# Moving five of the 24 depthwise-tap products of a band from VectorE to ScalarE and to adding transfers, in the last image of a two-layer convolution kernel

## The chip, the cores and the metric

The kernel runs on one core of one Trainium2 chip. The metric is the device time of one execution in microseconds (us), taken as the median of several runs. The engines are called by the profile's names: PE (TensorE, matrix products), ACT (ScalarE), DVE (VectorE), POOL (GpSimd), SP (SyncE, which here only issues transfers), and the DMA engines that move data.

## The reference

Eight images of 384 channels and 64 x 64 pixels pass through two layers, each added to its own input. Layer 0 is group normalisation and linear attention over the pixels. Layer 1, where the change lies, is

```
t  = w_in @ groupnorm(x)                       # 384 x 384, per pixel
t  = irfft2(rfft2(t, 8x8 patches) * filter)    # per channel
t  = depthwise 3x3 convolution of t with w_dw  # per channel, zero padding
x1, x2 = first and second half of the channels
x  = x + w_out @ (gelu(x1) * x2)
```

Everything is float32.

## The kernel before

**Tiling.** The channels are three tiles of 128 partitions (index `m`). An image is cut into eight bands of eight rows, so a band of one channel tile is 128 x 512 numbers. Layer 0 of image b + 1 and layer 1 of image b run interleaved through most of the program. The last image has nothing left to interleave: its layer 1 is a stage of its own, lines 1130 to 1150, and the change acts only there.

**One band of that stage** (loop variable `j`):

1. `expand_filter` (L688): PE makes `pi` (the product with `w_in`, L694), ACT copies it to `ht` (L701), PE makes the transform `pd` (L708), and DVE multiplies it by the filter into `tf` (L716).
2. `normalised` (L322): ACT prepares the next band's input `hf`.
3. `back_transform` (L719): PE makes `pb` from `tf` (L729), ACT copies it into `ring[j % 2]` (L739), a tile of ten rows of 66 columns for each channel. Row 0 is copied from the band above (L744), and row 9 of the band above is filled from this one (L745).
4. `first_taps` (L772): ACT makes the product of tap 0 for each `m` (L776) and so starts the band's sums, the tile `dw` (two buffers, pool `taps`).
5. `contract(b, j - 2)` (L852): PE makes `pw` from `gated` (L820, L831) and ACT copies it to `y` (L845). One transfer issued by POOL adds `y` to the output in memory (L850).
6. `taps(b, j - 1)` (L789): for the band before, DVE does the other eight taps of each `m` in `tile_taps` (L781), one instruction each (L787): `dw[m] = ring[m, shifted] * weight + dw[m]`. Taps 0 to 5 read rows 0 to 8 of the ring tile; taps 6 to 8 also read row 9, and so have to wait for the next band.
7. `gate_taps` (L795): gelu on ACT (L799, L803) and products on DVE (L800, L804) turn the sums into `gated`, a single buffer, which contraction j - 1 reads one iteration later.

In bands 6 and 7 (`on_array`, L751) the taps of `m` = 2 are done by PE as products with diagonal matrices (`ptap`, L764), and DVE does 16 taps.

**Order of the work.** Each engine works through its own queue strictly in order. The order inside a queue is fixed when the program is built: a planner plays the program through with its own estimates of every duration, and whenever an engine is free it takes the ready instruction that stands first in the program text. Scratch tiles (`w_tile`, nine buffers) and PSUM tiles (eight) are handed out in the order of the text. Where a real duration differs from the estimate, the engine does not choose again: it waits at the head of its queue.

Outside this stage, `tile_taps` is called by `last_band` and by `taps` through `depthwise_gate` for the other images.

Of the kernel before, what the change touches and what calls it, by code (L numbers as in the profile page):

```python
# [11 lines left out]
AF = mybir.ActivationFunctionType  # L12
ALU = mybir.AluOpType

P = 128
C = 384
CT = 3
# [100 lines left out]
def conv_blocks_kernel(ctx: ExitStack, tc: tile.TileContext, a: dict, out: bass.AP, nb: int):  # L118
    nc = tc.nc
# [9 lines left out]
    def ps_tile(name):  # L129
        return psum.tile([P, 512], F32, tag="ps", name=name)  # L130

    def w_tile(shape, name):
        return work.tile(shape, F32, tag="w", name=name)
# [13 lines left out]
    def store_x(b, j):  # L147

        if (b, j) != (nb - 1, NBAND - 1):
            nc.sync.dma_start(x_out[b][:, :, j * BT : (j + 1) * BT], xt.pop((b, j)))  # L150
# [79 lines left out]
    def const_tile(shape, name, src, queue=nc.scalar):  # L230
        t = const.tile(shape, F32, tag=name, name=name)
        queue.dma_start(t, src)
        return t
# [13 lines left out]
    scale = HD ** -0.5  # L247
# [9 lines left out]
    ring = []  # L257
# [64 lines left out]
    def normalised(b, j, params, order, name):  # L322

        rs, nb_ = params
        h = w_tile([P, CT, BT], f"h{name}_{b}_{j}")
        for t in range(CT):
            dst, src = h[:, t, :], xt[b, j][:, t, :]
            if order is not None:
                blocks, width = order
                dst = dst.rearrange("p (b r c) -> p r b c", b=blocks, r=8, c=width)  # L330
                src = src.rearrange("p (r b c) -> p r b c", b=blocks, r=8, c=width)
            nc.scalar.activation(dst, src, AF.Identity, bias=nb_[:, t : t + 1], scale=rs[:, t : t + 1])  # L332
        return h
# [354 lines left out]
    def expand_filter(b, j, h, done):  # L688
        ht = w_tile([P, 4, C], f"ht_{b}_{j}")
        tf = w_tile([P, 4, C], f"tf_{b}_{j}")  # L690
        for i in range(4):
            p_ = ps_tile(f"pi_{b}_{j}_{i}")
            for t in range(CT):
                nc.tensor.matmul(  # L694
                    p_[:, :C],
                    h[:, t, i * P : (i + 1) * P],
                    w_in[:, t, :],
                    start=(t == 0),
                    stop=(t == CT - 1),
                )  # L700
            nc.scalar.copy(ht[:, i, :], p_[:, :C])  # L701
        yield

        for s in range(2):
            p_ = [ps_tile(f"pd_{b}_{j}_{2 * s + i}") for i in range(2)]
            for above in range(2):
                for i in range(2):
                    nc.tensor.matmul(  # L708
                        p_[i][halves[above], :C],
                        dft[halves[i], :],  # L710
                        ht[halves[i], 2 * s + above, :],
                        start=True,
                        stop=True,
                    )
            for i in range(2):
                nc.vector.tensor_mul(tf[:, 2 * s + i, :], p_[i][:, :C], filt)  # L716
        done.append(tf)

    def back_transform(b, j, tf):  # L719
        t = ring[j % 2]  # L720
        for m0, m1 in ((0, 2), (2, 3)):


            ps = [ps_tile(f"pb_{b}_{j}_{m0}_{u}").rearrange("p (m s i n) -> p m s i n", m=2, s=2, i=2) for u in range(2)]
            for m in range(m0, m1):
                for k in range(4):
                    for c in range(2):
                        for u, half in enumerate(halves):
                            nc.tensor.matmul(  # L729
                                ps[u][halves[c], m - m0, k // 2, k % 2],  # L730
                                tf[half, k, m * P + 64 * c : m * P + 64 * c + 64],
                                idft[half, :],
                                start=True,
                                stop=True,
                            )
            for m in range(m0, m1):
                rows = t[:, m, 1:9, 1 : W + 1].rearrange("p r (s u i c) -> p u r s i c", s=2, u=2, i=2)
                for u in range(2):
                    nc.scalar.copy(rows[:, u], ps[u][:, m - m0].rearrange("p s i (r c) -> p r s i c", r=8))  # L739
        if j == 0:  # L740
            nc.gpsimd.memset(t[:, :, 0, :], 0.0)
        else:
            before = ring[(j - 1) % 2]
            nc.scalar.copy(t[:, :, 0, :], before[:, :, 8, :])  # L744
            nc.scalar.copy(before[:, :, 9, :], t[:, :, 1, :])  # L745
        if j == NBAND - 1:
            nc.gpsimd.memset(t[:, :, 9, :], 0.0)

    dw, dw_pe, diagonals = {}, {}, []

    def on_array(b, j):  # L751

        return b == nb - 1 and j >= NBAND - 2
# [7 lines left out]
    def array_taps(b, j, ks):  # L761

        for k in ks:
            nc.tensor.matmul(  # L764
                dw_pe[b, j].rearrange("p (r w) -> p r w", w=W),
                diagonals[0][:, k * P : (k + 1) * P],
                ring[j % 2][:, 2, k // 3 : k // 3 + 8, k % 3 : k % 3 + W],
                start=(k == 0),
                stop=(k == 8),
            )  # L770

    def first_taps(b, j):  # L772

        acc = dw[b, j] = taps_pool.tile([P, CT, 8, W], F32, tag="dw", name=f"dw_{b}_{j}")
        for m in range(CT - on_array(b, j)):
            nc.scalar.activation(acc[:, m], ring[j % 2][:, m, 0:8, 0:W], AF.Copy, scale=w_dw[:, m, 0:1])  # L776
        if on_array(b, j):
            dw_pe[b, j] = ps_tile(f"ptap_{b}_{j}")
            array_taps(b, j, range(9 if j == NBAND - 1 else 6))

    def tile_taps(b, j, m):  # L781

        t, acc = ring[j % 2], dw[b, j]
        for k in range(1, 9):
            src = t[:, m, k // 3 : k // 3 + 8, k % 3 : k % 3 + W]
            wd = w_dw[:, m, k : k + 1]
            nc.vector.scalar_tensor_tensor(acc[:, m], src, wd, acc[:, m], ALU.mult, ALU.add)  # L787

    def taps(b, j):  # L789
        if on_array(b, j) and j < NBAND - 1:  # L790
            array_taps(b, j, range(6, 9))
        for m in range(CT - on_array(b, j)):
            tile_taps(b, j, m)

    def gate_taps(b, j):  # L795
        g = gated
        af = dw.pop((b, j)).rearrange("p t r w -> p t (r w)")
        last = dw_pe.pop((b, j)) if on_array(b, j) else af[:, 2, :]
        nc.scalar.activation(g[:, :BT], af[:, 0, :], AF.Gelu)  # L799
        nc.vector.tensor_mul(g[:, :BT], g[:, :BT], af[:, 1, :])  # L800
        for h, gelu in enumerate((gelu2[64:P, :], g[64:P, BT:])):
            of = slice(h * HT, (h + 1) * HT)
            nc.scalar.activation(gelu, last[0:64, of], AF.Gelu)  # L803
            nc.vector.tensor_mul(g[halves[h], BT:], gelu, last[64:P, of])  # L804
# [47 lines left out]
    def contract(b, j):  # L852
        run(contraction(b, j))
# [18 lines left out]
    def run(*chains):  # L872

        chains = list(chains)
        while chains:
            chains = [c for c in chains if next(c, chains) is not chains]
# [135 lines left out]
    for c0, at, n in QRUNS:  # L1012

        t, p0, quarter, first = at // P, at % P, c0 // QC, c0 % QC
# [13 lines left out]
    w_dw = const_tile([P, CT, 9], "w_dw", a["w_dw"], nc.sync)  # L1028
# [31 lines left out]
    def last_band(b):  # L1060

        for m in range(CT):
            tile_taps(b, NBAND - 1, m)
            if m == CT - 1:
                gate_taps(b, NBAND - 1)
            yield
        if b + 1 < nb - 1:
            contract(b, NBAND - 1)

    before_last, late = nothing, iter(())  # L1070
    for b in range(nb):
# [19 lines left out]
        for j in range(NBAND):  # L1091
# [19 lines left out]
            some(2 * items)  # L1111
            back_transform(b, j, tf[0])
            first_taps(b, j)
            some(items)
            if j > 1:
# [15 lines left out]
    b = nb - 1  # L1131
    h = ahead
    for j in range(NBAND):
        tf = []
        layer1 = expand_filter(b, j, h, tf)
        run(layer1)
        store_x(b, j)
        if j < NBAND - 1:
            h = normalised(b, j + 1, params, (8, 8), "f")
        back_transform(b, j, tf[0])  # L1140
        first_taps(b, j)
        if j >= 2:
            contract(b, j - 2)
        if j >= 1:
            taps(b, j - 1)
            gate_taps(b, j - 1)
# [45 lines left out]
```

## Time and profile before

| what | value |
|---|---|
| time before, median of 3 runs | 3383.83 us (3383.71 to 3386.06) |
| the profiled execution's own time | 3384.08 us |
| its span, from first to last instruction | 3382.3 us |
| PE busy over the span | 3300.6 us (98%) |
| DVE busy | 2786.1 us (82%) |
| ACT busy | 1965.9 us (58%) |
| POOL busy | 142.6 us (4%) |
| L787 on DVE, whole program | 1520 instructions, 748 ns mean |
| first `pi` of the last image's layer 1 | 3203.78 us |
| first tap product of band 0 on ACT (L776) | 3219.83 us |
| the same of band 7 | 3350.67 us |

In the profile an instruction is named by its line, its engine and what it writes and reads (`dw<-ring,w_dw,dw`). Busy shares are averages over the whole span. The last image's stage is only the last 180 us, so what bounds it has to be read from views that are limited to it.

### The profile page before, as it was taken

What the parts mean: (1) busy time and instruction counts of PE and PEld (TensorE: products, weight loads), DVE (VectorE), ACT (ScalarE), POOL (GpSimd) and SP (SyncE); (2) the same over time, 40 slices, a digit from 0 to 9 for tenths busy, and PEclk for the clock granted to TensorE, in tenths of its full rate; (3) what the DMA queues carried; (4) which work ended last, traced back from release to release, by engine and by line L of the source; (5) the groups of instructions that cost most, each with busy time, mean ns of one, the idle gap of its engine ahead of it and who ended that gap; (6) DMA issues with size and microseconds to landing.
All of it is one profiled execution on the core that took longest, in us unless ns stands there. A gap on an engine that the chain in (4) does not pass through costs nothing.

```text
span 3382.3 us, 53235 instructions
## 1 busy us (share of the span) xinstructions
PE 3300.6 (98%) x21356; PEld 1850.2 (55%) x21356; DVE 2786.1 (82%) x4438; ACT 1965.9 (58%) x3849; POOL 142.6 (4%) x247
## 2 busy tenths in 40 slices
PE   8999999999999999999999999999999999999987
PEld 5544565456654566545664456644566445664454
DVE  6587889968899688996889868898788977989598
ACT  4445675556665576655675556655576555555553
POOL 0000001000010000100001000010000100000000
PEclk9999999999999999999999999999999999999999
DMA  6323244242442423424334333433233431324113
GB/s 223 112 94 108 75 101 111 100 138 56 111 115 94 135 74 87 123 101 120 85 89 122 102 115 76 111 109 116 92 96 93 120 114 54 85 70 112 57 24 53
DMA packets 149483, 336.01 MB, mean 99 GB/s; under 512 B 27140, under 2 KB 38388, under 8 KB 141044
## 3 DMA queue, kind: packets, MB, share of 16 engines
q1 hardware_dynamic: 123844, 282.85, 24.9%
q0 software_dynamic: 25200, 49.55, 10.1%
q8 instruction: 168, 2.75, 0.3%
q14 instruction: 79, 0.65, 0.1%
q10 hardware_dynamic: 192, 0.21, 0.0%
HBM read 232.70 MB, written 99.88 MB: 98 GB/s over the span
## 4 chain that ended last, share of the span: by engine, by line
PE 82%; DVE 14%; ACT 2%; issue 1%; DMA 0%; SPq 0%; DVEq 0%; ACTq 0%
PE pf L676 15%; PE pk L438 14%; PE pi L694 13%; PE pv L454 13%; PE pq L597 9%; DVE dw L787 6%; PE pw L820 4%; PE pb L729 3%; PE pd L708 2%; PE pw L831 2%; PE acc L470 2%; PE acc L483 2%; PE pn L635 1%; DVE qc L610 1%; DVE qc L339 1%
## 5 line engine op out<-in xcount | busy, mean ns | idle before, releaser
L787 DVE SCALAR_TENSOR_TENSOR dw<-ring,w_dw,dw 128x512 f32<-128x512 f32 x1520 | 1063.1, 748 | 244.2 <-ACT ring L745 205.4
L597 PE MATMUL pq<-x,wq 128*128 128x512 f32 x1152 | 529.0, 607 | 27.9 <-ACT qs L624 16.9
L438 PE MATMUL pk<-wk,x 128*128 128x384 f32 x1536 | 543.6, 495 | 0.0
L694 PE MATMUL pi<-w_in,hf 128*128 128x384 f32 x1536 | 514.4, 492 | 1.3 <-ACT hf L332 1.3
L676 PE MATMUL pf<-qc,mt 128*128 128x512 f32 x1152 | 512.8, 598 | 0.2
L454 PE MATMUL pv<-wv,x 128*128 128x384 f32 x1344 | 470.0, 488 | 0.0
L694 PEld LDWEIGHTS pi<-w_in,hf 128*128 128x128 f32 x1536 | 288.4, 191 | 196.0 <-issue 3.8
L438 PEld LDWEIGHTS pk<-wk,x 128*128 128x128 f32 x1536 | 282.9, 190 | 204.6 <-issue 31.3
L597 PEld LDWEIGHTS pq<-x,wq 128*128 128x128 f32 x1152 | 213.0, 192 | 278.9 <-issue 241.1
L461 ACT COPY v<-pv 128x384 f32<-128x384 f32 x224 | 108.7, 485 | 423.9 <-PE pv L454 416.3
L454 PEld LDWEIGHTS pv<-wv,x 128*128 128x128 f32 x1344 | 253.6, 190 | 181.4 <-issue 8.4
L676 PEld LDWEIGHTS pf<-qc,mt 128*128 128x128 f32 x1152 | 213.6, 190 | 253.7 <-issue 238.8
L680 DVE SCALAR_TENSOR_TENSOR x<-pf,bfc,x 128x512 f32<-128x512 f32 x192 | 140.8, 744 | 121.4 <-PE pf L676 121.3
L337 ACT ACTIVATE qs<-qc 128x1536 f32<-128x1536 f32 x64 | 95.0, 1485 | 169.7 <-DVE qc L626 148.6
L820 PE MATMUL pw<-gated,w_out 128*128 128x256 f32 x768 | 179.9, 384 | 0.0
L441 DVE TENSOR_TENSOR kc<-pk,kbias 128x384 f32<-128x384 f32 x256 | 141.0, 551 | 38.5 <-PE pk L438 38.2
L179 ACT ACTIVATE differences<-x,shift 128x512 f32<-128x512 f32 x168 | 119.7, 713 | 86.4 <-DVE x L680 86.4
L701 ACT COPY ht<-pi 128x384 f32<-128x384 f32 x256 | 115.0, 482 | 92.0 <-PE pi L694 88.7
L820 PEld LDWEIGHTS pw<-gated,w_out 128*128 128x128 f32 x768 | 146.9, 192 | 37.1 <-issue 6.5
L624 ACT ACTIVATE qs<-pq,qbias 64x512 f32<-64x512 f32 x128 | 87.4, 683 | 123.8 <-DVE qc L610 122.6
L850 POOL DMA_DIRECT2D out_dram<-y x63 | 80.7, 1281 | 1849.0 <-ACT y L845 847.1
L337 ACT ACTIVATE ks<-kc 128x1536 f32<-128x1536 f32 x64 | 95.0, 1485 | 98.6 <-DVE kc L445 69.5
(171 smaller groups left out, 4360.9 us busy)
## 6 DMA issues: line engine op xcount, KB each, us to landing
tq<-in_tq SPq DMA_DIRECT2D x64, 1024.0 KB, 4.8
x<-in_x SPq DMA_DIRECT2D x64, 768.0 KB, 5.9
tk<-in_tk SPq DMA_DIRECT2D x64, 768.0 KB, 4.4
out_dram<-x SPq DMA_DIRECT2D x63, 768.0 KB, 3.3
out_dram<-y POOLq DMA_DIRECT2D x63, 768.0 KB, 7.8
xs<-in_x SPq DMA_DIRECT2D x56, 768.0 KB, 5.9
wk<-in_wk SPq DMA_DIRECT2D x8, 576.0 KB, 3.8
wfc<-in_wfc SPq DMA_DIRECT2D x8, 576.0 KB, 7.9
```

The lines of the kernel that those rows point to most:

```text
L179: nc.scalar.activation(out[:, m, :], x_[:, m, :], AF.Identity, bias=shift[:, m : m + 1], accum_out=of_m[0])
L337: nc.scalar.activation(e, x_, AF.Relu, scale=-1.0)
L438: nc.tensor.matmul(pk[:, :C], tokens(t), wks[:, t, :], start=(t == 0), stop=(t == CT - 1))
L441: nc.vector.tensor_add(kc[:, i, :], pk[:, :C], bias)
L454: nc.tensor.matmul(pv[:, :C], xt[b, j][:, t, i * P : (i + 1) * P], wvs[:, t, :], start=(t == 0), stop=(t == CT - 1),)
L597: nc.tensor.matmul(p_, wqs[:, t, m * P : (m + 1) * P], xt[b, j][:, t, :], start=(t == 0), stop=(t == CT - 1),)
L676: nc.tensor.matmul(p_, mt[:, t, m * P : (m + 1) * P], q[:, t, :], start=(t == 0), stop=(t == CT - 1))
L680: nc.vector.scalar_tensor_tensor(xm, p_, bfc[:, m : m + 1], xm, ALU.add, ALU.add)
L694: nc.tensor.matmul(p_[:, :C], h[:, t, i * P : (i + 1) * P], w_in[:, t, :], start=(t == 0), stop=(t == CT - 1),)
L701: nc.scalar.copy(ht[:, i, :], p_[:, :C])
L787: nc.vector.scalar_tensor_tensor(acc[:, m], src, wd, acc[:, m], ALU.mult, ALU.add)
L820: nc.tensor.matmul(p_[h][:, m - m0, :], w_out[:, 0, m * P : (m + 1) * P], gated[:, h * HT : (h + 1) * HT], start=(m == m0), stop=False,)
```

## The change

For bands 0 to 5 of the last image, ACT also makes the products of tap 1 (all three `m`) and of tap 2 (`m` = 1 and 2), each into a scratch tile. Two transfers issued by POOL add these tiles onto the band's sums `dw`: the first adds three 128 x 512 tiles (768 KB), the second two (512 KB), onto bytes that the first has also written. DVE then starts at tap 2 for `m` = 0 and at tap 3 for `m` = 1 and 2, and does 19 instructions where it did 24.

```
+    first_on_vector = {}
+
+    def add_tap(b, j, k, m0):
+
+        t = w_tile([P, CT, 8, W], f"tap_{b}_{j}_{k}")
+        for m in range(m0, CT):
+            nc.scalar.activation(t[:, m], ring[j % 2][:, m, 0:8, k : k + W], AF.Copy, scale=w_dw[:, m, k : k + 1])
+            first_on_vector[b, j, m] = k + 1
+        nc.gpsimd.dma_start(out=dw[b, j][:, m0:], in_=t[:, m0:], accum_op=ALU.add)
+
     def first_taps(b, j):
...
     def tile_taps(b, j, m):
         t, acc = ring[j % 2], dw[b, j]
-        for k in range(1, 9):
+        for k in range(first_on_vector.pop((b, j, m), 1), 9):
...
         first_taps(b, j)
+        if not on_array(b, j):
+            for k in (1, 2):
+                add_tap(b, j, k, k - 1)
         if j >= 2:
             contract(b, j - 2)
```

The order of the text puts the new products and transfers after tap 0 of the band, ahead of `contract(b, j - 2)` and of the taps of the band before.

## The prediction

> **What bounds the stage now.** I read the page first (PE busy 98%), then limited views to the last stage, because the change touches nothing before 3219 us. The chain of waits from 3190 us on:
>
> ```profile
> by line: DVE dw L787 47.4%; PE pw L820 6.5%; DVE tf L716 5.8%; PE ptap L764 5.6%; PE pi L694 5.5%; PE pb L729 4.2%; ACT ring L739 3.7%; PE pw L831 3.1%; issue 3.0%; DVE gated L804 2.2%; DVE gated L800 2.1%; PE pf L676 1.1%; PE ps_r L281 0.8
> ...
> 3282.37 1.95 DVE tf L716 x4
> 3284.32 3.37 DVE dw L787 x6
> 3287.69 0.52 issue
> 3288.21 5.47 DVE dw L787 x9
> ...
> 3294.17 0.69 DVE gated L800
> 3294.86 7.29 DVE dw L787 x11
> 3302.15 1.40 DVE tf L716 x3
> ```
>
> From one `tf` to the next the chain never leaves DVE: here VectorE is the bound, not PE. The timeline of PE (start, duration, instruction, idle time before and its releaser) shows the same from the other side, PE waiting for `tf` before each `pb`, and the busy times of a window of one band (PE, PEld, DVE, ACT, POOL) show DVE full and ACT half empty:
>
> ```profile
> 3302.67 1.50 PE L729 MATMUL pb<-idft,tf 64*64 64x64 f32 x48 [2.10 <-DVE tf L716]
> ...
> 3287.40:3308.60 21.20, 19.09 (x167) 12.26 (x167) 21.11 (x35) 11.13 (x27) 1.28 (x1) 0.91 0.27 39
> ```
>
> Call R the start of a band's first L776. It is 3248.29 for band 2 and 3326.81 for band 6: 19.63 us a band.
>
> Prices, from groups and timelines of the stage and from the list of transfers:
>
> ```profile
> L787 DVE SCALAR_TENSOR_TENSOR dw<-ring,w_dw,dw 128x512 f32<-128x512 f32 x154 | 104.0, 749 | 4.7 <-ACT dw L776 3.3 <-ACT ring L745 1.0
> ...
> 3287.89 1.99 ACT L776 ACTIVATE dw<-ring,w_dw 128x512 f32<-128x512 f32 x3
> ...
> 3341.87 3.90 DVE L787 SCALAR_TENSOR_TENSOR dw<-ring,w_dw,dw 128x512 f32<-128x512 f32 x5
> ...
> tk<-in_tk SPq DMA_DIRECT2D x64, 768.0 KB, 4.4
> out_dram<-y POOLq DMA_DIRECT2D x63, 768.0 KB, 7.8
> ...
> q0 software_dynamic: 25200, 49.55, 10.1%
> ...
> DVE wv L352 <- DMA wv<-in_wv: 8.0, 7, 1.2
> ```
>
> Nine interleaved taps take 6.05 us (3256.49), so one costs (6.05 - 0.75) / 8 = 0.66; five that each need the one before cost (3.90 - 0.75) / 4 = 0.79. A product on ACT: (1.99 - 0.75) / 2 = 0.62. The only transfer that adds is `y`, 7.8 us to landing. Queue q0 carries just these: 10.1% of 16 engines x 3382 us over 63 transfers is 86.8 engine-us, or 5.4 us on 16 engines, so 2.4 us are fixed. The last line says the planner is optimistic on transfers: in seven images DVE reached the scaling of `wv` up to 1.2 us before the load had landed.
>
> **The Trainium skill.** "DMA: Bandwidth & Descriptors", section "Anatomy of one DMA", gives about 2 us of fixed cost; the trace's 2.4 agrees. The same page, "Rules for kernel authors", says that an accumulating transfer beside another access of the same bytes loses data unless it waits for the earlier one's semaphore. So the second add is issued only after the first has landed; nothing in this trace has two such adds. Its section "Queues, rings and completion order" says each DMA engine consumes descriptors in ring order, so a `y` transfer issued from POOL between the two adds goes ahead of the second; the trace doesn't show it, its `y`s being some 20 us apart. "SBUF — State Buffer", section "Who interferes with whom", says transfers don't contend with compute engines; I charge nothing.
>
> **The change, part by part.**
>
> Removed: five L787 in each of six bands, 5 x 0.66 = 3.3 us a band, 20 us in all, all of it on the chain above.
>
> Floors. DVE would need 19 x 0.66 + 1.95 (`tf`) + 0.6 (L800) + 0.9 (two L804) = 16.0, and about 1 more where fewer independent sums can be interleaved (0.79 for 0.66): 17. PE without waits: in band 7, where `tf` came promptly, `pi` to `pb` is 3336.19 to 3346.30 = 10.1, `pb` to `pw` 2.5, both parts of `pw` 2.7 + 1.5: 16.8. So at most 19.6 - 17 = 2.6 a band can be had.
>
> Added on ACT: 5 x 0.62 = 3.1 a band. 11.1 + 3.1 = 14.2 of 19.6: hidden. Queued behind the products are the four `y` copies and the next band's `ht`. `y` is done about 3 us later than now (R + 7.5), which only its transfer feels. `ht` comes every 1.93 us with 1.46 idle between, so ACT has caught up before the last `ht`, the one that `pd` waits for. Without this cover it would be up to 3 a band.
>
> Added on POOL: two issues at 1.28 (the L850 row); POOL is otherwise idle, but waits for the first add before it issues the second.
>
> Added waits, the heart of it. Tap 1 is done at R + 6 x 0.62 + 0.13 = R + 3.9. The first add moves as many bytes as `y`. Bounds: 4.4 to landing if adding cost nothing (the `tk` row, contiguous rows as here), 7.8 if it costs what it does into memory, more if adding into SBUF is slower than into memory. I take 7.0, as long rows save a little: landing R + 10.9. The second, two thirds of it: 3.3 to 6.0, I take 5.8: R + 16.7 alone. But `y` of band j - 2 is issued at R + 7.5, behind the first add and ahead of the second. The first add's packets end about 0.7 before its landing, at R + 10.2; `y` then takes its 5.4 to R + 15.6, the second add 5.4 x 2/3 = 3.6 to R + 19.2, landing R + 19.9. I take 19.9, range R + 12 to R + 25.
>
> Where the wait goes. DVE reaches `m` = 1 and 2 of a band only after the second landing. Before, the next thing after the gate of band j is `tf` of band j + 2 (L804, then L716, at 3281.9); I keep that order. From R(j): landing 19.9; six taps 3 to 5 of `m` = 1, 2 and nine taps 6 to 8 of all, 15 x 0.66 + 3 x 0.13 = 10.3; gate 2.0; four taps of `m` = 0 of the next band, 4 x 0.73 = 2.9 (they are ready and go in while `pd` is made); `tf` to R, 5.3 (5.0 and 5.5 at 3321.82 and 3282.37). The sum, 40.4, is R(j + 2) - R(j): 20.2 a band, not 19.6. The 3.3 us saved are waited away. Over the four steady bands +0.6 x 4 = +2.4.
>
> Start. Before, DVE did 12 taps of band 0 from 3220.6 on and then `tf` of band 1 at 3228.69. Now no tap of band 0 is possible before 3219.83 + 10.9 = 3230.7. If the planner, optimistic, has one tap of `m` = 0 ahead of that `tf`, it starts at 3230.7 + 0.7 = 3231.4, +2.7; if not, -1.4, as PE's wait of 1.41 before `pb` goes. I take +2.7. Band 2 comes +1.5: twelve taps of band 0 stand behind its second landing, 3219.83 + 16.7 = 3236.5 (no `y` yet), until 3244.5, with `tf` of band 2 among the last.
>
> End. From R(7) on PE and DVE do what they did (22 taps, no adds): 0.
>
> Sum: 2.7 + 1.5 + 2.4 = +6.6. The profiled execution, 3384.08, becomes 3390.7; it lies 0.25 above the median of the runs, so 3390.5, say **3391 us**.
>
> **Rivals.**
>
> A. *Faster: the adds land in time.* If the second lands by about R + 15, DVE never finds them missing and a band takes 17.0 to 18.2, DVE's own work plus some unevenness. At 17.8: -1.8 x 4, and -1.4 at the start: -8.6, 3375. At PE's floor throughout it is -1.4 - 2.8 x 4 = -12.6, 3371. For it: the `tk` row, a same-sized move in 4.4. Against it: `y`'s measured 7.8, and the serial wait.
>
> B. *Much slower: `tf` stands behind a waiting tap.* DVE's order is fixed with the planner's estimates. If those land the second add about 4 us too early, one or more taps of `m` = 1 or 2 of band j stand ahead of `tf` of band j + 1, and PE, with nothing else ready, waits for a transfer in every band: 19.9 + 0.7 + 5.3 = 25.9, or 22.8 with no `y` in the way; at 24.5, +4.9 x 5 = +24, 3408. For it: the `wv` line, and serial transfers add their errors up. Against it: in the planner's play too DVE is busy with the band before until about R + 12, and a ready `tf` goes first. It decides from the first tap that stands ahead.
>
> C. *No difference.* The loop above equals 19.6 when the second add lands 1.2 us earlier, R + 18.7; with `tf` of band 1 first, the sum is about 0 to +3. Both are well inside my bounds.
>
> **Chances.** Forecast's loop, +1 to +14: 0.45 (0.20 of it below +0.2%). A: 0.29 (0.24 beyond -0.2%, the rest within). B, and slower transfers, over +14: 0.20. C: 0.06. I count 0.2%, 6.8 us, as what a measurement of this kernel tells from no change. Faster 0.24, same 0.05 + 0.20 + 0.06 = 0.31, slower 0.25 + 0.20 = 0.45. The range leaves out a tenth on each side: A's floor below -9, 3375, and B's worse half above +24, 3408. The forecast's own range is 3385 to 3398.
>
> **What will show it.** Right: idle time of DVE before L787 released by a transfer into `dw`, 2 to 4 us in most bands; landings of the adds near 7 and, behind `y`, 9; R at steps of about 20; PE's wait before `pb` as before or longer. Wrong: no such wait and PE's wait near 0.65 (A); `tf` right after a waiting tap, steps over 22 (B). An add into SBUF of 4 us, or of over 9, would move me to A or B; so would a different order of `tf`.

## The result and the profile after

The changed kernel takes 3410.18 us (median of 6 runs, 3406.34 to 3412.47) where the kernel before, run beside it, takes 3383.94 us (3383.59 to 3386.45): a ratio of 1.0074, 95% interval 1.0063 to 1.0084. The forecast was 3391 us, with a range up to 3408. The sign is right; the loss is 26 us where 6.6 were forecast, so the size, and the case behind it, are wrong. One execution of the run `e7_from_band2` below fell into a slow state (3814.57 us, clock 0.847) and is left out of its ratio. In the profiled execution (3408.59 us, span 3406.8 us) the lines of code below L771 stand 10 further down: L787 is now L797, L776 is L786.

From the first tap product of band 0 to that of band 7 the stage took 153.22 us where it took 130.84: 22.4 us more. What comes after the first tap product of band 7 takes as long as before (31.3 and 31.7 us). The first tap product itself starts at 3222.32 us, not 3219.83. Over the profiles of this study whose code up to there is the same (all but e11), that time lies anywhere between 3218.91 and 3223.92, so these 2.5 us are not put down to the change.

| from R of band ... to the next (us) | 0 | 1 | 2 | 3 | 4 | 5 | 6 | sum |
|---|---|---|---|---|---|---|---|---|
| before | 13.84 | 14.62 | 21.67 | 17.93 | 21.20 | 17.72 | 23.86 | 130.84 |
| after | 16.02 | 19.38 | 19.38 | 25.20 | 23.82 | 24.64 | 24.78 | 153.22 |

Bands 2 to 5 together, the steady ones, lost 14.5 us (93.04 for 78.52), bands 0 and 1, the start, 6.9, and band 6 0.9.

The chain of waits of the changed kernel from 3190 us on, start and duration of each piece:

```profile
by line: DMA dw<-tap 16.5%; DVE dw L797 11.8%; issue 9.7%; PE ptap L764 8.1%; PE pb L729 4.9%; PE pw L830 4.9%; ACT ring L739 3.8%; PE pi L694 3.7%; DVE tf L716 3.1%; PE pw L841 2.6%; ACT tap L778 2.3%; ACT dw L786 1.8%; POOL out_dram L860 
...
3312.91 7.00 DMA dw<-tap
3319.92 0.03 issue
3319.94 0.75 DVE dw L797
3320.70 0.48 DVE tf L716
3321.17 0.04 issue
3321.22 2.81 PE pb L729 x74
```

Before, VectorE's taps held 47% of this chain, and no transfer stood in that line. Now the largest single part is the adding transfer (`tap` is the scratch tile that it adds). The last six lines are one band: a transfer of 7.00 us, one tap that needed it, then `tf`, then `pb`. The timeline of VectorE for the same band (start, duration, what, how many, idle time before and its releaser):

```profile
3309.40 0.69 DVE L810 TENSOR_TENSOR gated<-gated,dw 128x512 f32<-128x512 f32 x1 [0.62 <-ACT gated L809]
...
3312.65 3.12 DVE L797 SCALAR_TENSOR_TENSOR dw<-ring,w_dw,dw 128x512 f32<-128x512 f32 x4 [1.65 <-DMA dw<-tap]
3319.94 0.75 DVE L797 SCALAR_TENSOR_TENSOR dw<-ring,w_dw,dw 128x512 f32<-128x512 f32 x1 [4.18 <-DMA dw<-tap]
3320.61 1.95 DVE L716 TENSOR_TENSOR tf<-pd,filt 128x384 f32<-128x384 f32 x4
```

VectorE has finished the gate of band 3 and four taps of `m` = 0 of band 4. Then it stands for 4.18 us before a single tap of `m` = 1 or 2, and `tf` of band 5, ready all that time, comes right behind it. PE, in the same band:

```profile
3313.72 1.52 PE L708 MATMUL pd<-ht,dft 64*64 64x384 f32 x16
3321.22 3.38 PE L729 MATMUL pb<-idft,tf 64*64 64x64 f32 x96 [5.98 <-DVE tf L716]
3324.52 3.80 PE L830 MATMUL pw<-gated,w_out 128*128 128x256 f32 x12
```

`pd` is done at 3315.24, and PE does nothing for 5.98 us; before, this wait was 2.10 us. The busy times of this band (PE, PEld, DVE, ACT, POOL, then clock, share of DMA, GB/s) and the list of transfers of the stage:

```profile
3302.30:3326.12 23.82, 17.84 (x161) 11.91 (x160) 16.79 (x26) 13.85 (x32) 3.03 (x3) 0.86 0.51 90
```

```profile
out_dram<-y POOLq DMA_DIRECT2D x8, 768.0 KB, 8.1
dw<-tap POOLq DMA_DIRECT2D x6, 768.0 KB, 5.8
dw<-tap POOLq DMA_DIRECT2D x6, 512.0 KB, 7.2
```

No engine is full any more: VectorE is busy for 16.8 of 23.8 us. The band is a chain of hand-overs. The taps themselves are no slower beside the transfers: over the stage one takes 749 ns on average, as before, so nothing was to be charged for that.

### The profile page after: what moved, and what is told of

Read it like the earlier page. It is cut to its first block, busy times and chain, and to the rows that moved or that the text cites. A ratio compares the mean times of both kernels' runs of the same rounds, so it can differ in the third digit from the quotient of the medians.

```text
span 3406.8 us, 53270 instructions
## 1 busy us (share of the span) xinstructions
PE 3307.1 (97%) x21356; PEld 1855.7 (54%) x21356; DVE 2769.2 (81%) x4408; ACT 1981.9 (58%) x3879; POOL 153.6 (5%) x259
## 5 line engine op out<-in xcount | busy, mean ns | idle before, releaser
L797 DVE SCALAR_TENSOR_TENSOR dw<-ring,w_dw,dw 128x512 f32<-128x512 f32 x1490 | 1046.8, 749 | 277.4 <-ACT ring L745 206.5
L597 PE MATMUL pq<-x,wq 128*128 128x512 f32 x1152 | 530.7, 608 | 29.3 <-ACT qs L624 16.7
```

The source lines that it names most:

```text
L597: nc.tensor.matmul(p_, wqs[:, t, m * P : (m + 1) * P], xt[b, j][:, t, :], start=(t == 0), stop=(t == CT - 1),)
```

## The experiments

Theory: the fixed order of VectorE has a tap that needs the second add ahead of `tf`, so PE waits for a transfer once a band. Rivals: the loop through the second landing costs it in any order; `y`, ahead of the second add in the queue, makes it late; ScalarE's extra products delay something. Runs e1 to e4, e5 to e8 and e9 to e12 each stand beside their own runs of the kernel before (medians 3385.78, 3385.99 and 3385.81 us, about 2 us above the first ones), so the ratios compare better than the medians; the last column is from one profiled execution each. Where the intervals of two runs overlap, their times alone show no difference.

| run | median us | ratio to before, 95% interval | R of band 0 to 7, us |
|---|---|---|---|
| e1_tf_first | 3389.11 | 1.0010 (1.0003 to 1.0017) | 137.10 |
| e2_y_behind | 3404.44 | 1.0056 (1.0041 to 1.0071) | 150.28 |
| e3_both | 3387.47 | 1.0004 (0.9995 to 1.0012) | 132.94 |
| e4_no_adds | 3383.71 | 0.9995 (0.9986 to 1.0004) | 130.08 |
| e5_no_adds_tf | 3369.65 | 0.9954 (0.9940 to 0.9969) | 116.82 |
| e6_act_only | 3387.14 | 1.0001 (0.9992 to 1.0010) | 130.74 |
| e7_from_band2 | 3384.07 | 0.9995 (0.9988 to 1.0002) | 130.20 |
| e8_all_from_band1 | 3379.74 | 0.9983 (0.9977 to 0.9990) | 126.82 |
| e9_before_all | 3392.47 | 1.0019 (1.0011 to 1.0027) | 135.34 |
| e10_after_from_band2 | 3403.72 | 1.0057 (1.0040 to 1.0073) | 149.34 |
| e11_ht_first | 3383.10 | 0.9992 (0.9983 to 1.0001) | 128.02 |
| e12_one_add | 3381.86 | 0.9990 (0.9981 to 0.9998) | 128.09 |

### Only VectorE's order changed

`issue_after` queues what its block writes behind one instruction of the same engine. In the traces PE, ScalarE and POOL work in the same order as in the changed kernel; only VectorE's order differs.

```
-                nc.vector.tensor_mul(tf[:, 2 * s + i, :], p_[i][:, :C], filt)
+                last_tf[b, j] = nc.vector.tensor_mul(tf[:, 2 * s + i, :], p_[i][:, :C], filt)
...
-            taps(b, j - 1)
+            if on_array(b, j - 1):
+                taps(b, j - 1)
+            else:
+                tile_taps(b, j - 1, 0)
+                with tc.issue_after(last_tf[b, j].ins):
+                    for m in (1, 2):
+                        tile_taps(b, j - 1, m)
```

> Only the order on VectorE is changed: the taps of m = 1 and 2 of band j - 1 are queued behind the last tf of band j; products, transfers and the number of taps stay. Theory 1 (a tap that waits for the second add stands ahead of tf): the three steps from the first tap product of band 3 to that of band 6, 25.2, 23.8 and 24.6 us, fall to about 18.5 each, so 18 us less: 3392 us (3386 to 3397), and PE's waits before pb shrink from about 6 us to under 2. Theory 2 (the loop through the second landing costs it, in whatever order): steps stay above 23 us, 3405 us or more.

Measured: 3389.11 us; the three steps are 18.06, 20.51 and 18.45 us. With 30 products on ScalarE and twelve adds unchanged, 3.3 of the 26 us are left. In the profiled stage 6.3 of the 22.4 us are left: the start still loses 7.2, band 6 1.2, and bands 2 to 5 take 2.1 us less than before. In the step of 20.51 us PE also waited 1.87 us for `ht`. The timeline of VectorE in this run shows the wait still there, behind `tf` instead of ahead of it:

```profile
3284.08 3.11 DVE L797 SCALAR_TENSOR_TENSOR dw<-ring,w_dw,dw 128x512 f32<-128x512 f32 x4
3287.11 1.95 DVE L716 TENSOR_TENSOR tf<-pd,filt 128x384 f32<-128x384 f32 x4
3292.78 10.28 DVE L797 SCALAR_TENSOR_TENSOR dw<-ring,w_dw,dw 128x512 f32<-128x512 f32 x15 [3.72 <-DMA dw<-tap]
...
3310.19 10.28 DVE L797 SCALAR_TENSOR_TENSOR dw<-ring,w_dw,dw 128x512 f32<-128x512 f32 x15 [0.62 <-DMA dw<-tap]
```

VectorE still idles 3.72 us for the transfer of band 3 and 0.62 for that of band 4, but PE has its `tf` by then. The rival "in whatever order" falls.

### y behind the second add

```
-        nc.gpsimd.dma_start(out=dw[b, j][:, m0:], in_=t[:, m0:], accum_op=ALU.add)
+        last_add[b, j] = nc.gpsimd.dma_start(out=dw[b, j][:, m0:], in_=t[:, m0:], accum_op=ALU.add)
...
-            contract(b, j - 2)
+            if on_array(b, j):
+                contract(b, j - 2)
+            else:
+                with tc.issue_after(last_add[b, j].ins):
+                    contract(b, j - 2)
```

> Only the order on POOL is changed: the transfer of y of band j - 2 is issued behind the second add of band j; VectorE keeps a tap that needs the second add ahead of tf. The second add should land at R + 14.5 instead of R + 17.8. Theory 1 (the stall is what tf waits for, so each us of landing counts once a band): 3.2 us less in each of three steps, 10 us less: 3400 us (3396 to 3404). If y ahead of the second add is the main cause: below 3390 us. If the landing does not matter: 3410 us.

Measured: 3404.44 us, 0.4 above what the theory gave (3396 to 3404). The list of transfers of this run:

```profile
dw<-tap POOLq DMA_DIRECT2D x6, 768.0 KB, 5.7
dw<-tap POOLq DMA_DIRECT2D x6, 512.0 KB, 4.6
```

The second add takes 4.6 us to landing alone. In the changed kernel the median of 7.2 mixes two adds without a `y` ahead (4.7 and 4.5 in bands 0 and 1) and four behind one, 7.0 to 8.2: `y` ahead of it costs 2.4 to 3.6 us. The waiting tap came at R + 15.5 in band 4 (3314.70), not R + 17.6, so 2.1 us earlier and not 3.2; the three steps fell to 22.53, 22.95 and 22.56, 5.6 us in all, while bands 1 and 2 grew by 2.5. A secondary cause.

### Both

The two diffs above together.

> Both orders changed: taps of m = 1 and 2 behind tf, and y behind the second add. Theory 1: the order has taken most of it, and the earlier landing adds about 1 us a band, by the loop over two bands (14.5 + 10.3 + 2.0 + 2.9 + 5.3 = 35 us, 17.5 a band): 3388 us (3381 to 3394). If the two causes were independent: 18 + 10 us less, 3382 us. If the transfers cost it in whatever order: above 3400 us.

Measured: 3387.47 us, as the theory had it. Once `tf` is first, the earlier landing is worth less: 2.3 us over the same three steps, where alone it was worth 5.6. Between the medians of this run and the first it is 1.6 us, within the intervals.

### Products without transfers

The line of the adding transfer is left out, so five of 27 tap products of six bands are missing from the output. The second run has VectorE's order of the first experiment as well.

> ScalarE still makes the five products of each of six bands, but the transfers that add them are left out, so five of 27 tap products are missing from the sums of these bands; VectorE does 19 taps. Theory 1 (the waits for the transfers are the whole loss): the steps fall to 17 to 18 us, and the kernel is faster than before by 8 to 14 us: 3370 to 3376 us. If ScalarE's extra products are what costs (ht, y and row copies late): at 3384 us or above, with PE waiting for ht or VectorE for the ring's rows.

Measured: 3383.71 us. A miss: with no transfer to wait for, and five taps fewer a band, the kernel is as fast as before, with steps of 19.81, 19.39, 19.25 and 18.94 us. VectorE does wait for the ring's row 9, 2.3 to 3.2 us a band, one of the two signs named for ScalarE's products; but in the next run, with the same products, that wait is gone.

> As the run without the adding transfers (ScalarE's five products of six bands are made and never added, so they are missing from the sums), with the order of the run that put tf first. Theory 1a (without the transfers the floor is PE's own 16.8 to 17.5 us a band, and what held the run without the adds at 19 to 20 us was ready taps ahead of tf): steps of 17.5 to 18.2 us, 3376 to 3380 us. Theory 1b (the floors of the forecast are too low: a band takes about 19 us with both engines' hand-overs counted, so the change had next to nothing to win): within 2 us of the run without the adds, 3382 to 3386 us.

Measured: 3369.65 us, below both of the ranges given, and steps of 16.75, 16.29, 16.30 and 16.29 us. ScalarE's products are in both. VectorE's timeline of the first of them, and of the second:

```profile
3315.33 4.73 DVE L796 SCALAR_TENSOR_TENSOR dw<-ring,w_dw,dw 128x512 f32<-128x512 f32 x7
3319.97 1.94 DVE L716 TENSOR_TENSOR tf<-pd,filt 128x384 f32<-128x384 f32 x4
```

```profile
3294.63 1.54 DVE L796 SCALAR_TENSOR_TENSOR dw<-ring,w_dw,dw 128x512 f32<-128x512 f32 x2
3296.18 1.95 DVE L716 TENSOR_TENSOR tf<-pd,filt 128x384 f32<-128x384 f32 x4
```

Seven taps, all ready, stood ahead of `tf` in the one and two in the other, and PE's wait before `pb` went from 1.99 us to none that the timeline shows:

```profile
3295.20 1.52 PE L708 MATMUL pd<-ht,dft 64*64 64x384 f32 x16
3296.79 2.55 PE L729 MATMUL pb<-idft,tf 64*64 64x64 f32 x96
```

So a ready instruction ahead of `tf` costs as a waiting one does, only less. The five taps removed are worth 14.0 us in the stage if `tf` is prompt, and 0.8 if it is not.

### ScalarE's products alone

The change with the adding transfer and the entry in `first_on_vector` left out: VectorE makes all 24 taps, and the products are unused.

> VectorE does all its 24 taps as before; ScalarE makes the five extra products of each of six bands, and they are used by nothing. If ScalarE's extra work is hidden: within 2 us of the kernel before, 3384 to 3388 us. If it delays ht, y or the row copies that VectorE waits for: up to 3.1 us a band in six bands, 3390 to 3402 us.

Measured: 3387.14 us, ratio 1.0001. The products are hidden on ScalarE, as the forecast costed them.

### Where the adds are made, and how much stands behind tf

First adds from band 2 on, with both orders as above for the same bands; then from band 1 on, with the taps of `m` = 0 behind `tf` too.

```
-        if not on_array(b, j):
+        if 2 <= j < NBAND - 2:
             for k in (1, 2):
                 add_tap(b, j, k, k - 1)
```

> Both orders changed as in the run with both, and the adds are made for bands 2 to 5 only; bands 0 and 1 are as in the kernel before. If the start of the stage is what still held that run (its bands 1 to 2 took 20.2 us where before they took 14.6, with VectorE waiting 12.4 us for the first adds): the steps of bands 0 to 2 go back to 13.8 and 14.6 us, and the kernel is 5 to 7 us faster than with the adds in all six bands: 3380 to 3383 us. If the start is not it: 3387 us.

Measured: 3384.07 us, above the 3380 to 3383 expected. It is 3.4 less than with both orders and all six bands, though the intervals overlap; in the stage of the two profiles it is 2.7. The steps of bands 0 and 1 are 13.84 and 14.08 us again, but band 2 takes 22.45: of 7.7 us gained at the start, 3.2 come back there.

```
-        if not on_array(b, j):
+        if 1 <= j < NBAND - 2:
...
-                tile_taps(b, j - 1, 0)
                 with tc.issue_after(last_tf[b, j].ins):
-                    for m in (1, 2):
-                        tile_taps(b, j - 1, m)
+                    taps(b, j - 1)
```

> Adds for bands 1 to 5, y behind the second add, and all taps of band j - 1, those of m = 0 too, queued behind the last tf of band j. Worked out: 15 taps, gate and then tf, so R to R is 9.9 + 1.7 + 5.3 = 16.9 us for VectorE's part and 16.8 to 17.5 us for PE's; with the start as before (13.8, 15) the time from band 0 to band 7 is 122 to 126 us where before it was 130.8: 3377 to 3381 us. If the floor is nearer 19 us a band: no gain, 3384 us or more.

Measured: 3379.74 us, ratio 0.9983 (0.9977 to 0.9990): faster than both kernels, by 6.2 us than the one before. Bands 2 to 5 take 20.26, 16.53, 18.54 and 17.42 us. One thing left in them is another hand-over of the same kind, on ScalarE, where the last `ht` stands behind gelus that wait for VectorE. PE's timeline in band 2:

```profile
3259.18 1.51 PE L708 MATMUL pd<-ht,dft 64*64 64x384 f32 x12
3263.15 1.40 PE L708 MATMUL pd<-ht,dft 64*64 64x384 f32 x4 [2.46 <-ACT ht L701]
```

### The same order without the change

The kernel before, with `last_tf` as above and the taps of bands 1 to 5 behind it.

> The kernel before, with no product or transfer moved, but with the order that gave the fastest version: for bands 1 to 5 all taps of band j - 1 stand behind the last tf of band j. If that order alone made the gain of 6 us: 3379 to 3381 us. If VectorE's 24 taps bound the kernel before, as the forecast has it (24 x 0.66 + 3.5 = 19.3 us a band), the order has nothing to win there: 3384 to 3390 us.

Measured: 3392.47 us, ratio 1.0019: slower than before by 6.7 us, and above the 3384 to 3390 expected. From band 0 to band 6 the stage takes as long as before (107.3 and 107.0 us), with VectorE busy for 103.7 of it: with 24 taps it is full, and the order has nothing to give. The loss lies in band 6, 28.06 us for 23.86, and behind it; its cause there is open. The order and the smaller number of taps win only together.

### The start alone

The changed kernel with adds from band 2 on and nothing else changed.

> The changed kernel with the planner's own order, and the adds made for bands 2 to 5 only; bands 0 and 1 as before. Theory: the start is a loss of its own. Bands 0 to 3 took 54.8 us in the changed kernel and 50.1 before, so 4 to 7 us come back: 3403 to 3406 us, while the steps from band 3 to band 6 stay at 24 to 25 us. If the start is no separate loss, or moves into the later steps: 3410 us. If the stalls hang on the start: below 3395 us.

Measured: 3403.72 us, inside the theory's 3403 to 3406; the steps from band 3 on are 24.27, 23.87 and 24.47 us. The start was a loss of its own, 6 us between the medians and 4 in the stage of the profiles, and the stalls don't hang on it.

### Two attempts to better it

`pi` and `ht` of the next band are written ahead of the gate, and the two small gelus queued behind the last `ht`:

```
-    def gate_taps(b, j):
+    def gate_taps(b, j, after=ExitStack):
...
-            nc.scalar.activation(gelu, last[0:64, of], AF.Gelu)
+            with after(): nc.scalar.activation(gelu, last[0:64, of], AF.Gelu)
...
+        if j < NBAND - 1:
+            layer1 = expand_filter(b, j + 1, h, tf)
+            next(layer1)
...
+                gate_taps(b, j - 1, lambda: tc.issue_after(last_ht[b, j + 1].ins))
```

> The run with all taps behind tf, adds for bands 1 to 5, and on ScalarE the two gelus of 64 x 256 of band j - 1 queued behind the last ht copy of band j + 1 (pi and ht are written in the text ahead of the gate for that). In that run pd waited 2.46 and 1.19 us for an ht that stood behind a gelu. If that wait is what its bands still lose: 2 to 5 us less, 3375 to 3378 us. If VectorE's gate, now later, stands ahead of tf and gives it back: 3379 us or more.

Measured: 3383.10 us, 3.4 more than without, between the medians, but the intervals overlap (0.9983 to 1.0001 and 0.9977 to 0.9990): a gain is not shown, nor a loss. From band 3 to band 7 it takes 77.35 us, without it 77.36: what PE gained on `ht` it lost to `tf`, which now stood behind gate products that waited for the later gelus. One line of VectorE's timeline shows it, at 3287.45, just ahead of `tf`:

```profile
3287.45 0.42 DVE L814 TENSOR_TENSOR gated<-gelu,dw 64x256 f32<-64x256 f32 x1 [2.50 <-ACT gelu L813]
3287.91 0.42 DVE L814 TENSOR_TENSOR gated<-gated,dw 64x256 f32<-64x256 f32 x1
3288.36 1.95 DVE L716 TENSOR_TENSOR tf<-pd,filt 128x384 f32<-128x384 f32 x4
```

Band 2 is 2.2 us longer besides; the second add of band 1, for which VectorE waited 4.77 us, landed at R + 16.8 instead of R + 15.2, and why it did is open.

With only tap 1 moved (`for k in (1,):`), one add a band and 21 taps:

> The run with all taps behind tf, for bands 1 to 5, but with only tap 1 moved to ScalarE (three products, one add of 768 KB; VectorE does 21 taps). If in that run the second add's landing no longer matters and VectorE's taps do, two taps more cost 0 to 1.3 us in each of five bands: 3380 to 3386 us. If waiting for two adds in a row is still what it loses: 3375 to 3378 us.

Measured: 3381.86 us, 2.1 more than with both taps moved, inside what was expected if VectorE's taps matter and the second landing no longer does; but the two intervals overlap, so a difference is not shown.

## Why the prediction was wrong

**The step that failed** is "I keep that order" under "Where the wait goes". From it came the loop over two bands, 40.4 us, and with it +2.4 for the four steady bands; they took +14.5. VectorE's queue did not keep that order once `dw` came from transfers: in bands 3, 4 and 5 one tap that needs the second add stands ahead of `tf` of the next band, and PE waits for both. Band 4 is shown above; bands 3 and 5:

```profile
3295.45 0.75 DVE L797 SCALAR_TENSOR_TENSOR dw<-ring,w_dw,dw 128x512 f32<-128x512 f32 x1 [5.11 <-DMA dw<-tap]
3296.12 1.02 DVE L716 TENSOR_TENSOR tf<-pd,filt 128x384 f32<-128x384 f32 x2
...
3343.92 0.75 DVE L797 SCALAR_TENSOR_TENSOR dw<-ring,w_dw,dw 128x512 f32<-128x512 f32 x1 [4.75 <-DMA dw<-tap]
3344.59 1.01 DVE L716 TENSOR_TENSOR tf<-pd,filt 128x384 f32<-128x384 f32 x2
```

These three steps took 16.8 us more than before; with the order assumed, in the first experiment, they took 57.02 us, as before (56.85). This is rival B, to which I gave 0.20 together with other causes, and which "decides from the first tap that stands ahead": one did. B's arithmetic with the measured landing is 17.6 + 0.7 + 5.3 = 23.6 us for band 4, and 23.82 were measured. That B's total, +24, lies near the measured loss is partly luck: it had five stalled steps and no loss at the start, where three steps stalled and the start lost 6.9. (Its 22.8 is 22.7 by its own terms.) My argument against B, that a ready `tf` goes first in the planner's play too, holds only if the landing is played as late as it is. What landing the planner assumed is not on record; only the order that it made is, and that could be read before the program ran.

**The loop itself was right.** In the first experiment, where the order is what I assumed, the second add releases VectorE at R + 18.75 in band 3 and R + 18.10 in band 4. The prediction's other terms, 10.3 + 2.0 + 2.9 + 5.3, give 38.9 us on a mean of 18.4; measured are 38.57 us from band 3 to 5 and 38.96 from band 4 to 6. But that this run's loss is of the forecast's order is luck: its steady bands took 2.1 us less than before, not 2.4 more, and the start 7.2 more, not 4.2.

**Transfers: too slow in the forecast, and it did not matter.** The first add landed in 5.8 us, not 7.0, and each second add was issued 0.3 to 0.6 us after that. The second, behind a `y`, released its tap at R + 18.4, 17.6 and 17.8 in bands 3, 4 and 5, not 19.9. By rival C the loop breaks even at R + 18.7, so with my order the steady bands would have lost nothing, as the first experiment shows. That `y` goes ahead in the ring was right: 7.0 to 8.2 us against 4.6. The Trainium skill ("DMA: Bandwidth & Descriptors", section "Queues, rings and completion order") states the ring order where it describes SP's and ACT's queues; the trace agrees for POOL's: in band 4 the packets of `y` start from 3311.78 to 3316.96 us, those of the second add from 3316.26 to 3319.30.

**Start.** "+2.7" was +2.2: one tap of `m` = 0 ahead of `tf` of band 1, after a wait of 12.40 us. "Band 2 comes +1.5" was +4.8: after a second landing that came earlier than I had it (R + 15.0, not R + 16.7), I had twelve taps of band 0 ahead of `tf` of band 2, the trace has eighteen taps and the gate's first product.

```profile
3232.17 0.75 DVE L797 SCALAR_TENSOR_TENSOR dw<-ring,w_dw,dw 128x512 f32<-128x512 f32 x1 [12.40 <-DMA dw<-tap]
...
3237.44 10.40 DVE L797 SCALAR_TENSOR_TENSOR dw<-ring,w_dw,dw 128x512 f32<-128x512 f32 x15 [2.00 <-ACT ring L739]
3247.76 0.69 DVE L810 TENSOR_TENSOR gated<-gated,dw 128x512 f32<-128x512 f32 x1
3248.36 2.07 DVE L797 SCALAR_TENSOR_TENSOR dw<-ring,w_dw,dw 128x512 f32<-128x512 f32 x3
3250.34 1.48 DVE L716 TENSOR_TENSOR tf<-pd,filt 128x384 f32<-128x384 f32 x3
```

**Floors.** PE without waits was put at 16.8 us a band; without the adds and with `tf` prompt it ran at 16.3. So more was to be had than my 2.6 us a band, but 19 taps alone did not give it (3383.71 us). Rival A, adds in time, was put at 8.6 us; the run nearest to it, without any adds and in the planner's order, won 2 us, within the noise. I counted the work of each engine and not the place of `tf` among it.

**Right:** the products hidden on ScalarE (ratio 1.0001), the end unchanged (-0.4 behind R of band 7; band 6, for which the sum had no term, took +0.9), and what would show B: `tf` right after a waiting tap, steps over 22.

**Not costed:** a wait of PE can make its next matmuls slow as well. The band that the profile after shows, the same work in the run without adds, and in the kernel before, each from the start of `pb` to the end of `pw`:

```profile
3321.22:3329.75 8.53, 8.53 (x121) 6.98 (x121) 8.18 (x14) 5.75 (x14) 0.00 (x0) 0.69 0.01 2
```

```profile
3296.79:3303.60 6.81, 6.67 (x121) 5.19 (x121) 6.81 (x12) 5.67 (x14) 0.00 (x0) 1.00 0.29 53
```

```profile
3302.67:3310.99 8.32, 8.30 (x121) 6.11 (x121) 8.23 (x15) 5.78 (x15) 0.00 (x0) 0.79 0.01 3
```

The same 121 matmuls take 8.53 us at a clock of 0.69, 6.81 at 1.00, and 8.32 at 0.79. So a wait of 5.98 us cost about 1.7 more after it than no wait, but only 0.2 more than the wait of 2.10 us that the kernel before had in its place: this explains little of the loss. Over the whole stage PE was busy 5.4 us longer than before and idle 17.0 us longer.

The Trainium skill ("TensorE: Matmul & The Clock Gate", section "HAM oscillation — how this bites in real kernels") speaks of gaps of more than about 3.4 us that let the clock drop to half. Here it dropped after shorter ones too: in the kernel before, after the waits of 2.10 to 2.77 us in four bands, to 0.78 or 0.79 on average over the matmuls behind them. Two waits of the first experiment show that the length of a wait alone does not settle it here:

```profile
3308.23 2.55 PE L729 MATMUL pb<-idft,tf 64*64 64x64 f32 x96 [1.86 <-DVE tf L716]
...
3326.21 3.33 PE L729 MATMUL pb<-idft,tf 64*64 64x64 f32 x96 [1.75 <-DVE tf L716]
```

Behind the longer wait the clock was 1.00, behind the shorter 0.73. What else decides it is open.

## What to carry to other kernels

When work is moved behind a transfer in a kernel whose queues are ordered by estimates, first ask which instruction the bound engine waits for and what the new order puts ahead of it; here one waiting tap a band ahead of `tf` cost 16.8 us over three bands. Free time on an engine is worth something only if the instruction that another engine waits for gets it, so count the place of that instruction and not only the busy time; the fewer taps and the new order each gained nothing alone (3383.71 and 3392.47 us), and together they did. Put what is due next ahead by a dependency instead of trusting the estimate, and leave the first band, where nothing covers the transfer, as it was.

## What was not expected of the hardware

The adds into `dw`, in the chip's own memory, landed sooner than `y`'s add into `out_dram`: 768 KB took 5.8 us to landing where `y` took 7.8 in the kernel before, and an add of 512 KB, alone, 4.6. The pieces differ too (6144 bytes for the first add, 2048 for `y`), so how much is due to the memory stays open. POOL's issue of an add took 0.86 to 0.90 us, of `y` 1.28. The clock in the stage fell with PE's waits: 0.88 with the stalls of the changed kernel, 0.95 before, 1.00 in the run without adds and with `tf` prompt; over the stage the same 1082 matmuls kept PE busy for 118.93, 113.51 and 109.33 us.
